# Layer 0 self attention: queries and keys from seven block products a step instead of eight, with sums formed in PSUM

## The chip, the cores and the metric

One core of a Trainium2 chip runs the whole kernel. The metric is the device time of one execution in microseconds (us). Five engines matter: TensorE (PE in the profile, its weight loads PEld), VectorE (DVE), ScalarE (ACT), GpSimd (POOL) and SyncE (SP), which issues the transfers. Each works through its own list of instructions in order and waits on semaphores where it needs another's result. PSUM has eight banks of 512 fp32 columns; TensorE writes them, VectorE and ScalarE read them, and ScalarE can write them too.

## The reference

Two transformer layers over 16 sequences of 256 tokens with 256 features, all fp32. The part that the change touches is the self attention of layer 0: 16 heads of 64, rotary positions, no mask.

```
q = _heads(xq @ wq)
k, v = jnp.split(ctx @ wkv, 2, axis=-1)
...
q = _rope(q, sq, cq)
k = _rope(k, sk, ck)
sim = jnp.einsum('bhnd,bhmd->bhnm', q, k) * DH ** (-0.5)
a = jax.nn.softmax(sim, axis=-1)
o = jnp.einsum('bhnm,bhmd->bhnd', a, v)
return o @ wo + bo
```

In self attention `ctx` is `xq`, the normalized and modulated input, so queries and keys are both a product of the same 256 x 256 activations with 256 x 1024 weights.

## The kernel before, in words

Six phases follow each other: layer 0 self attention, cross attention, feed forward, then the same three of layer 1. A phase has one job for each of the 16 sequences. A layer 0 attention job has two steps, s = 0 and s = 1 (called the even and the odd step here); a step handles eight heads, as two groups of four (u = 2s and 2s + 1, or e = 0 and 1). The loop runs over all steps, and the order of every engine's instructions is the order in which the program issues them (a manual schedule), so a line that stands earlier in the loop body is ahead on its engine.

A step of layer 0 self attention, in the order of TensorE:

1. Scores (`scores`, L1057, and `stage_s`, L585; matmuls at L598) of this step into banks 0 to 3 (e = 0) and 4 to 7 (e = 1). ScalarE takes four exponentials (L610) out of them into `pr`.
2. Queries and keys of the next step (`stage_rotary`, L539, through `product`, L77, whose matmul is L82): for each of four pairs (e, half) one bank holds 256 columns of q and 256 of k. `product` cuts the 128 output rows into four strips of 32, which TensorE works on side by side. Each bank is multiplied on VectorE with cosines and with sines (L555, two instructions of 512 columns), and once both halves of an e are there, GpSimd joins them into `qk` (L563, two instructions of 512 columns). The products `m0` and `m1` have two buffers each.
3. Attention-weighted values (`layer0_sums`, L659, matmuls L667), copied out by ScalarE (L674).
4. In the even step the values of the next job (`layer0_values`, L487, 64 matmul instructions of 512 columns); in the odd step the output projection of the job before (`finish_folded`, L946), which already works with seven block products of 128 columns and adds its results onto x on VectorE (L958, L959, L961, L964, L965). It uses banks 4 and 5.

VectorE also sums the exponentials (`stage_t`, L619: the two key halves of `pr`, both in SBUF, are added; `stage_turn`, L625, a transpose; `stage_reduce`, L632), and does the normalization of a later job (L349 to L373). GpSimd also scales the attention results (`scale`, L656, four instructions of 512 columns, in the even step), forms five sums for the output projection (`fold_inner`, L944: three in the even step after `scale`, two in the odd step between the two pairs of L563), adds a bias (L451) and half of the input's affine (L425). One fp32 matmul of the program shows as two instructions in the profile.

Weights: `wk0`, `wq0`, `wk1`, `wq1` hold the two halves of the key and query weights, `wo` the output weights (two slots under this tag). `load_phase(p, part)` issues a phase's loads by parts; the output weights belong to "early", which for phase p + 1 is issued in the second job of phase p.

Of the kernel before, what the change touches and what calls it, by code (L numbers as in the profile page):

```python
# [10 lines left out]
F32 = mybir.dt.float32  # L11
I32 = mybir.dt.int32
AF = mybir.ActivationFunctionType
ALU = mybir.AluOpType
AX = mybir.AxisListType

P = 128
# [26 lines left out]
def fast(ctx: ExitStack, tc: tile.TileContext, a: dict, out: bass.AP, flag):  # L44
# [222 lines left out]
    def wtile(shape, tag, name, bufs=1):  # L267
        return wpool.tile(shape, F32, tag=tag, name=name, bufs=bufs)
# [4 lines left out]
    def load_layer0_attention(kind, part, between=None):  # L273
        halves = [slice(i * 512, (i + 1) * 512) for i in range(4)]
        wkv_src = chunked(a[f"{kind}_wkv"])
        w = {}
        if part in ("first", "last"):
            i = ("first", "last").index(part)
            wk, wq = (wtile([P, 2, 512], f"w{n}{i}", f"w{n}{i}_{kind}") for n in "kq")
            nc.sync.dma_start(out=wk, in_=wkv_src[:, :, halves[i]])  # L280
            nc.sync.dma_start(out=wq, in_=chunked(a[f"{kind}_wq"])[:, :, halves[i]])
            w[f"wk{i}"], w[f"wq{i}"] = wk, wq
            if between is not None and i == 0:
                between()
        if part == "values":
            w["wv"] = wtile([P, 2, H * 64], "wv", f"wv_{kind}")
            for i in range(2):
                nc.sync.dma_start(out=w["wv"][:, :, halves[i]], in_=wkv_src[:, :, halves[2 + i]])
        if part == "early":
            w["bo"] = broadcast_row(a[f"L0_xcond_{kind}_bo"], "bo", f"bo_{kind}")  # L290
            w["wo"] = wtile([P, 8, D], "wo", f"wo_{kind}", 2)
            nc.sync.dma_start(out=w["wo"], in_=chunked(a[f"{kind}_wo"]))
        return w
# [245 lines left out]
    def stage_rotary(job, u, half, first_bank):  # L539
# [18 lines left out]
        if half == 1:  # L558
            (even_cos, even_sin), (odd_cos, odd_sin) = job["turns"]
            job["turns"] = []  # L560
            for out, (x, y) in enumerate(((even_cos, odd_sin), (odd_cos, even_sin))):
                r = work.tile([P, 2, N], F32, tag="qk", name=f"qk_{key}_{u}_{out}", bufs=4)
                nc.gpsimd.tensor_tensor(r, x, y, (ALU.subtract, ALU.add)[out])  # L563
                job["qk"].setdefault(u, []).append(r)

    def stage_a(job, c, at):

        w, key = job["phase"]["w"], job["key"]
        cut = slice(c * P, (c + 1) * P)
        pq = bank(at, 2, N)  # L570
        for s, (wt, src) in enumerate(((w["wq"], job["hT"]), (w["wk"], job["kT"]))):
            for k in range(2):
                product(pq[:, s, :], wt[:, k, cut], src[:, k, :], k == 0, k == 1)
        q = work.tile([P, N], F32, tag="ctx", name=f"q_{key}_{c}")
        nc.vector.tensor_scalar(q, pq[:, 0, :], w["bq"](c), None, ALU.add)

        k1 = work.tile([P, 2, N], F32, tag=("both", "squares")[c], name=f"k_{key}_{c}", bufs=1)
        nc.vector.scalar_tensor_tensor(
            k1, pq[:, 1:2, :].to_broadcast([P, 2, N]), w["bk"](c),
            mask[:, 0:2].rearrange("p (e o) -> p e o", o=1).to_broadcast([P, 2, N]), ALU.add, ALU.mult,  # L580
        )
        for e in range(2):
            job["qk"][2 * c + e] = (q, k1[:, e, :])

    def stage_s(job, u, at):  # L585

        key = job["key"]
        pair = job["qk"].pop(u)
        for t in range(NT):
            for half in range(2 if job["layer"] == 0 else 1):  # L590
                for g, h in [(g, h) for g in range(2) for h in range(4)]:
                    r = slice(32 * h, 32 * h + 32)
                    keys = slice(t * P + 64 * g, t * P + 64 * g + 64)
                    if job["layer"] == 0:
                        lhs, rhs = pair[half][r, 1, keys], pair[half][r, 0, :]
                    else:
                        lhs, rhs = pair[1][r, keys], pair[0][r, :]
                    nc.tensor.matmul(  # L598
                        banks[64 * g : 64 * g + 64, at + h, t * N : (t + 1) * N], lhs, rhs,
                        start=(half == 0), stop=(half == 1 or job["layer"] == 1),  # L600
                    )
        prs = []
        for p in range(2):
            pr = work.tile([P, 2, NT, N], F32, tag="pr", name=f"pr_{key}_{u}_{p}", bufs=4)
            sc = banks[:, at + 2 * p : at + 2 * p + 2, :].rearrange("p h (t n) -> p h t n", n=N)

            parts = 2 if job["layer"] == 1 and u % 2 == 0 and p == 0 else 1
            for i in range(parts):
                one = slice(i, i + 1) if parts == 2 else slice(0, 2)
                nc.scalar.activation(pr[:, one], sc[:, one], AF.Exp, scale=0.125 if job["layer"] == 0 else 0.25)  # L610
            prs.append(pr)
        job["pr"][u] = prs
# [43 lines left out]
            nc.gpsimd.tensor_tensor(part, part, spread[:, u : u + 1, :].to_broadcast([P, 2, N]), ALU.mult)  # L656
            job["parts"].append(part)

    def layer0_sums(job, u, at):  # L659

        key, v, prs = job["key"], job["v"], job["pr"].pop(u)
        o = bank(at, 2, N)
        for half in range(2):
            for t in range(NT):
                for h in range(4):
                    col = (4 * u + h) * 64 + 32 * half
                    nc.tensor.matmul(  # L667
                        o[32 * h : 32 * h + 32, half, :], v[:, t, col : col + 32], prs[h // 2][:, h % 2, t, :],
                        start=(t == 0), stop=(t == NT - 1),
                    )  # L670
        if u % 2 == 0:
            job["halves"].append(work.tile([P, 4, N], F32, tag="part", name=f"raw_{key}_{u}", bufs=4))
        raw = job["halves"][-1][:, 2 * (u % 2) : 2 * (u % 2) + 2, :]
        nc.scalar.copy(raw, o)  # L674
        job["raw"].append(raw)
# [267 lines left out]
            folded[m] = work.tile([P, 4, P], F32, tag="folded", name=f"folded_{job['key']}_{m}", bufs=5)  # L943
            eng.tensor_tensor(folded[m], *sums[m])  # L944

    def finish_folded(job, at):  # L946

        x, weights, hidden = xs[job["b"]], job["phase"]["folded"], job.pop("folded")
        hurry = len(at) == 3
# [3 lines left out]
        for m in (3, 6, 4, 5, 2, 1, 7) if hurry else places:  # L953
# [7 lines left out]
        nc.vector.tensor_tensor(  # L961
            square, first[:, 2:4, :].unsqueeze(1).to_broadcast([P, 2, 2, P]), square, ALU.add
        )
        nc.vector.tensor_tensor(outer, third[:, 0:1, :].to_broadcast([P, 2, P]), outer, ALU.add)  # L964
        nc.vector.tensor_tensor(outer, second[:, 1:3, :], outer, ALU.add)  # L965
        if job["last"]:
# [90 lines left out]
    def scores(i):  # L1057

        at0, at1 = attention(i, 0), attention(i, 1)
        if at0:  # L1060
            for e in range(2):
                stage_s(at0[0], 2 * at0[1] + e, 4 * e)
        if at1:
            for e in range(2):
                stage_s(at1[0], 2 * at1[1] + e, 4 * ((e + at1[1]) % 2))
        then = attention(i + 1, 0)
        if then and then[0]["cross"]:
            for e in range(2):
                start_keys(then[0], 2 * then[1] + e, 2 * e)
# [5 lines left out]
    phases[0]["make_mod"] = phases[0]["mod_load"]()  # L1075
    load_x(0)
    nc.sync.dma_start(out=rows, in_=a["rows"])
    for part in ("first", "last", "early"):
        load_phase(0, part)
    for b in range(3, NB):  # L1080
        load_x(b)
# [26 lines left out]
    add_bias(jobs[0])  # L1108
    prepare_moments(jobs[2])
    prepare_norm(jobs[2])  # L1110
    prepare_input(jobs[1])
    for i, (j, s) in enumerate(steps):
        job = jobs[j]
        ffn, layer0 = job["kind"] == "ffn", job["layer"] == 0
# [13 lines left out]
        leaving = layer0 and not ffn and job["b"] == NB - 1  # L1128
        if layer0 and not ffn and job["b"] == NB - 2 and s == 1:
            load_phase(job["p"] + 1, "values")  # L1130
        if leaving and s == 0:
            load_phase(job["p"] + 1, "first")
        if layer0 and not ffn and s == 1 and job["b"] == 2:
# [100 lines left out]
        elif layer0:  # L1234
            then = attention(i + 1, 0)
            if leaving and s == 1 and nxt["kind"] == "ffn":
                fold_input_weights(nxt["phase"], nc.gpsimd)
            stage_t(job, 2 * s, 0)
            stage_t(job, 2 * s, 1)
            stage_turn(job, 2 * s)  # L1240
            rotary(then, 0, 0)
            stage_t(job, 2 * s + 1, 0)
            rotary(then, 0, 1)
            if late is not None and s == 1 and then:
                fold_inner(late, nc.gpsimd, 7, 6)
            if late is not None and s == 0:
                sum_up(late, 6)
            if make_mod:
                make_mod["mod"] = make_mod["make_mod"](6)
            stage_t(job, 2 * s + 1, 1)  # L1250
            rotary(then, 1, 0)
            rotary(then, 1, 1)
            if leaving and s == 0:
                load_phase(job["p"] + 1, "last")
            for e in range(2):
                layer0_sums(job, 2 * s + e, 4 + e if then else e)
            stage_reduce(job, 2 * s)
            stage_turn(job, 2 * s + 1)
            stage_reduce(job, 2 * s + 1)
            if late is not None and s == 1:  # L1260
                if then:
                    finish_folded(late, (4, 5))
                else:
                    finish(late, 7)
            if late is not None and s == 0:
                scale(late)
                if nxt["kind"] == "attn":
                    fold_inner(late, nc.gpsimd, 5, 2, 1)
            if nxt["kind"] == "attn" and s == 0:
                layer0_values(nxt)  # L1270
            if s == 0:
                prepare_moments(third)
                context_moments(third)
                prepare_fetch(after)
            else:
                prepare_norm(third)
                prepare_context(third)
                prepare_input(after)
# [652 lines left out]
```

## Time and profile before

| | us |
|---|---|
| Runs of the kernel before | 2176.7, 2177.61, 2177.8; median 2177.61 |
| The profiled execution's own time | 2174.7 |
| Its span, from first to last instruction | 2172.9 |
| Granted TensorE clock, mean | 0.999 |
| First and last matmul with `wk_sa` (layer 0 self attention) | 12.3 and 649.3 |

The profile lists busy times by engine, groups of instructions by line, a timeline, and the chain of work that ended last. In a row, "x128" is a count, "128x512" partitions by columns, and what stands after "<-" in brackets is what ended the engine's idle time. A matmul row's busy time overlaps with its neighbours', since matmuls are pipelined; where a duration of a stretch of matmuls is needed, it is taken from one start to the next.

### The profile page before, as it was taken

The page shows a single profiled execution, that of the slowest core. Times are in us where ns is not written, and L with a number is a line of the kernel's source. Part 1 is how long each engine was busy: PE and PEld are TensorE (multiplying, and loading weights), DVE is VectorE, ACT ScalarE, POOL GpSimd, SP SyncE. Part 2 cuts the span into 40 slices and gives each one's busy share as a digit, 9 for nine tenths or more (in the row PEclk, how much of TensorE's full clock was granted, in tenths as well). Part 3 has the DMA queues.
Part 4 walks back from the last instruction along what each step waited for, and adds up shares of the span by engine and source line. Part 5 has one row for each costly group of instructions (what it writes and reads, how often), then busy time and mean ns, then how long its engine had stood idle before and what let it go on. Part 6 is the DMA issues. An engine that isn't in the chain of part 4 may idle for free.

```text
span 2172.9 us, 110193 instructions
## 1 busy us (share of the span) xinstructions
PE 2154.7 (99%) x50112; PEld 1437.1 (66%) x50112; DVE 1688.5 (78%) x3108; ACT 870.1 (40%) x1362; POOL 1240.9 (57%) x1174
## 2 busy tenths in 40 slices
PE   9999999999999999999999999999999999999998
PEld 5666666666665666666666667998556665656787
DVE  6876777777888889888889887774777777777875
ACT  3323233233233233332333334443666666664432
POOL 3766656656657867677676767662232323235673
PEclk9999999999999999999999999999999999999999
DMA  6110010011123221121211123221211232223221
GB/s 194 49 38 22 23 42 22 23 29 36 27 74 86 66 58 44 42 60 35 61 41 44 43 62 99 56 44 25 64 43 39 48 102 63 59 48 78 74 64 39
DMA packets 307030, 117.69 MB, mean 54 GB/s; under 512 B 243364, under 2 KB 289784, under 8 KB 306424
## 3 DMA queue, kind: packets, MB, share of 16 engines
q1 hardware_dynamic: 306008, 110.02, 20.5%
q8 instruction: 394, 6.46, 1.3%
q14 instruction: 84, 0.69, 0.1%
q10 hardware_dynamic: 544, 0.52, 0.1%
HBM read 77.14 MB, written 33.29 MB: 51 GB/s over the span
## 4 chain that ended last, share of the span: by engine, by line
PE 92%; POOL 2%; DVE 2%; DMA 2%; issue 1%; SPq 1%; ACT 0%; DVEq 0%; POOLq 0%; ACTq 0%
PE banks L82 59%; PE banks L598 16%; PE banks L667 9%; PE banks L683 5%; PE banks L534 1%; PE banks L501 1%; POOL raw L656 1%; DMA spread<-sums_seen 0%; DVE m L555 0%; DMA fetched<-turned 0%; DMA sums_seen<-inv 0%; SPq L388 0%; POOL qk L563 0%; POOL folded L944 0%; POOL folded L869 0%
## 5 line engine op out<-in xcount | busy, mean ns | idle before, releaser
L610 ACT ACTIVATE pr<-banks 128x1024 f32<-128x1024 f32 x576 | 487.4, 937 | 415.3 <-PE banks L598 211.9
L563 POOL TENSOR_TENSOR qk<-m,m 128x512 f32<-128x512 f32 x256 | 347.8, 1379 | 302.6 <-DVE m L555 210.7
L555 DVE TENSOR_TENSOR m<-banks,rope 128x512 f32<-128x512 f32 x512 | 324.2, 679 | 85.7 <-POOL qk L563 81.4
L619 DVE TENSOR_TENSOR both<-pr 128x512 f32<-128x512 f32 x256 | 218.9, 867 | 107.9 <-ACT pr L610 107.5
L674 ACT COPY raw<-banks 128x512 f32<-128x512 f32 x128 | 75.2, 587 | 467.3 <-PE banks L667 443.1
L598 PE MATMUL banks<-qk 32*64 32x256 f32 x8192 | 240.7, 377 | 3.0 <-DVE x L961 1.8
L667 PE MATMUL banks<-pr,v 128*32 128x256 f32 x4096 | 233.2, 379 | 0.0
L598 PEld LDWEIGHTS banks<-qk 32*64 32x64 f32 x8192 | 184.1, 131 | 63.7 <-issue 22.4
L667 PEld LDWEIGHTS banks<-pr,v 128*32 128x32 f32 x4096 | 132.9, 110 | 88.7 <-ACT pr L610 0.7
L656 POOL TENSOR_TENSOR raw<-raw,spread 128x512 f32<-128x512 f32 x128 | 162.7, 1304 | 19.7 <-DMA spread<-sums_seen 19.3
L725 POOL TENSOR_TENSOR oT<-oT,spread 128x256 f32<-128x256 f32 x64 | 45.8, 737 | 206.0 <-DVE spread L724 206.0
L625 DVE STREAM_TRANSPOSE squares<-both 128x1024 f32<-128x1024 f32 x128 | 159.4, 1246 | 4.4
L632 DVE TENSOR_REDUCE rows<-squares 128x32 f32<-128x1024 f32 x128 | 155.4, 1214 | 2.2
L451 POOL TENSOR_TENSOR x<-x,bo_b 128x256 f32<-128x256 f32 x96 | 73.0, 781 | 121.2 <-DVE xh L363 121.2
L82 PE MATMUL banks<-hT,wk_sa 128*32 128x256 f32 x2048 | 134.7, 381 | 0.0
L683 PE MATMUL banks<-pr,wide_v 128*32 128x256 f32 x2048 | 134.3, 379 | 0.0
L82 PE MATMUL banks<-hT,wq_ca 128*32 128x256 f32 x2048 | 133.9, 379 | 0.0
L82 PE MATMUL banks<-hT,wq_sa 128*32 128x256 f32 x2048 | 133.9, 379 | 0.0
L355 POOL TENSOR_TENSOR rstd<-ve,neg_half 128x2 f32<-128x2 f32 x95 | 73.0, 769 | 101.0 <-DVE ve L353 97.6
L944 POOL TENSOR_TENSOR folded<-raw,raw 128x512 f32<-128x512 f32 x90 | 127.8, 1448 | 2.4
L900 DVE TENSOR_TENSOR x<-banks,x 128x256 f32<-128x256 f32 (+2 forms) x150 | 79.7, 531 | 63.2 <-PE banks L82 57.0
L598 PE MATMUL banks<-q,k 32*64 32x256 f32 x4096 | 127.8, 381 | 0.0
(225 smaller groups left out, 4020.8 us busy)
## 6 DMA issues: line engine op xcount, KB each, us to landing
turned<-blocks SPq DMA_DIRECT2D x380, 64.0 KB
fetched<-turned SPq DMA_DIRECT2D x380, 64.0 KB
spread<-sums_seen SPq DMA_DIRECT2D x128, 128.0 KB
x<-in_x SPq DMA_DIRECT2D x16, 256.0 KB
fetched_c<-turned_c SPq DMA_DIRECT2D x64, 64.0 KB
cT<-in_ctx_turned SPq DMA_DIRECT2D x16, 256.0 KB
out<-x SPq DMA_DIRECT2D x15, 256.0 KB
ctx<-in_ctx SPq DMA_DIRECT2D x16, 192.0 KB
```

Source lines behind the costliest of these rows:

```text
L82: nc.tensor.matmul(out[cut], lhsT[:, cut], rhs, start=start, stop=stop, **more)
L555: nc.vector.tensor_tensor(m, pq, rope[:, s : s + 1, :].to_broadcast([P, 2, N]), ALU.mult)
L563: nc.gpsimd.tensor_tensor(r, x, y, (ALU.subtract, ALU.add)[out])
L598: nc.tensor.matmul(banks[64 * g : 64 * g + 64, at + h, t * N : (t + 1) * N], lhs, rhs, start=(half == 0), stop=(half == 1 or job["layer"] ...
L610: nc.scalar.activation(pr[:, one], sc[:, one], AF.Exp, scale=0.125 if job["layer"] == 0 else 0.25)
L619: nc.vector.tensor_tensor(job["both"][:, 2 * p : 2 * p + 2, :], pr[:, :, 0, :], pr[:, :, 1, :], ALU.add)
L625: nc.vector.transpose(job["squares"].rearrange("p b k -> p (b k)"), job.pop("both").rearrange("p h n -> p (h n)"))
L632: nc.vector.tensor_reduce(job["rows"][:, u, :], job.pop("squares"), AX.X, ALU.add)
L656: nc.gpsimd.tensor_tensor(part, part, spread[:, u : u + 1, :].to_broadcast([P, 2, N]), ALU.mult)
L667: nc.tensor.matmul(o[32 * h : 32 * h + 32, half, :], v[:, t, col : col + 32], prs[h // 2][:, h % 2, t, :], start=(t == 0), stop=(t == NT - 1),
L683: nc.tensor.matmul(o[32 * h : 32 * h + 32], v[:, t, 4 * c + h, 32 * e : 32 * e + 32], prs[h // 2][:, h % 2, t, :], start=(t == 0), stop=(t ...
L944: eng.tensor_tensor(folded[m], *sums[m])
```

## The change

For the steps of layer 0 self attention of jobs 1 to 15 (30 steps; job 0 keeps the old way for its own two), the product of 256 tokens x 256 features with 256 features x 256 columns is done as a 2 x 2 block product with seven instead of eight products of 128 x 128 blocks, for each of two halves of q and of k.

- `fold_projections` forms the weight sums: 8 instructions of 128x512 for a step index, once; for s = 0 on GpSimd ahead of the loop, for s = 1 on VectorE in the odd step of job 0. The sum `low[0] + low[1]` replaces a part of the weights in place.
- `fold_tokens` forms four sums of 128x128 of a job's input on GpSimd, in the even step of the job before, ahead of `scale`.
- `begin_seven` issues products 1 and 5 (banks 0 and 1) right after the scores, and ScalarE copies bank 0 to bank 2 between the third and the fourth exponential. The other products are added onto banks 0, 1 and 2 in the order 2, 6, 7, 4, 3, between the quarters of `layer0_sums`. `keep_sum` (ScalarE) copies bank 2 to SBUF after product 6 and after product 7; `add_fifth` (VectorE) adds bank 1 to each copy.
- `rotate` replaces the rotary part: again two VectorE instructions of 128x512 for each of four pieces, but a piece is now one token half of one e. Two pieces come from PSUM (banks 0 and 2), two from the SBUF copies. GpSimd joins each piece with two instructions of 128x256.
- The scores start their PSUM accumulation once in a bank instead of twice. In the odd step `stage_reduce` of the second group moves between the third and the fourth of the five additions of `finish_folded`. `sum_up` comes after product 6, and `fold_inner` 7 and 6 stand ahead of all `rotate` work on GpSimd.
- `sums_of_weights` takes the second slot of `wo`, so the output weights of the cross attention are loaded by a new part "output" in the odd step of job 15 instead of job 1.

```diff
+    def fold_projections(ph, s, eng):
...
+            eng.tensor_tensor(s3[:, i], top[0], low[0], ALU.subtract)
+            eng.tensor_tensor(low[0], low[0], low[1], ALU.add)
+            eng.tensor_tensor(s2[:, i], low[0], top[0], ALU.subtract)
+            eng.tensor_tensor(s4[:, i], top[1], s2[:, i], ALU.subtract)
...
+    def fold_tokens(job, eng):
...
+        eng.tensor_tensor(t1, b[0][1], b[0][0], ALU.subtract)
+        eng.tensor_tensor(t2, b[1][1], t1, ALU.subtract)
+        eng.tensor_tensor(t3, b[1][1], b[0][1], ALU.subtract)
+        eng.tensor_tensor(t4, b[1][0], t2, ALU.subtract)
...
+    def seven(job, s, m, place, start=False):
+        for i, n in enumerate("qk"):
+            a = job["phase"]["projections"][s][n][m]
+            for half in range(2):
+                product(
+                    place[:, 2 * i + half, :], a[:, half * P : (half + 1) * P], job["tokens"][m],
+                    start and i == 0 and half == 0, True, skip_group_check=True,
+                )
+    def begin_seven(job, s):
+        first, fifth, chain = (bank(i, 4, P) for i in range(3))
+        seven(job, s, 1, first, True)
+        seven(job, s, 5, fifth, True)
+        nc.scalar.copy(chain, first)
+    def keep_sum(job, s, i):
...
+            kept = work.tile([P, 4, P], F32, tag="cT", name=f"kept{i}_{key}_{s}")
+        nc.scalar.copy(kept, bank(2, 4, P))
+        return kept
+    def add_fifth(kept):
+        nc.vector.tensor_tensor(kept, bank(1, 4, P), kept, ALU.add)
+    def rotate(job, s, e, t, src):
...
+        for i in range(2):
+            m = work.tile([P, 4, P], F32, tag=f"m{i}", name=f"m{i}_{key}_{u}_{t}")
+            nc.vector.tensor_tensor(m, src, rope[:, i : i + 1, t * P : (t + 1) * P].to_broadcast([P, 4, P]), ALU.mult)
...
+        for i, r in enumerate(job["qk"][u]):
+            nc.gpsimd.tensor_tensor(
+                r[:, :, t * P : (t + 1) * P], cos[:, i], sin[:, 1 - i], (ALU.subtract, ALU.add)[i]
+            )
...
-            stage_t(job, 2 * s, 0)
-            stage_t(job, 2 * s, 1)
-            stage_turn(job, 2 * s)
-            rotary(then, 0, 0)
-            stage_t(job, 2 * s + 1, 0)
-            rotary(then, 0, 1)
...
+            if by_seven(then):
+                ahead = then
+                first, fifth, chain = (bank(n, 4, P) for n in range(3))
+                for p in range(2):
+                    stage_t(job, 2 * s, p)
+                stage_turn(job, 2 * s)
+                if late is not None and s == 1:
+                    fold_inner(late, nc.gpsimd, 7, 6)
...
+                stage_t(job, 2 * s + 1, 0)
+                layer0_sums(job, 2 * s, 4, (0,))
+                seven(*ahead, 2, first)
+                rotate(*ahead, 0, 0, first)
+                seven(*ahead, 6, chain)
+                two = keep_sum(*ahead, 0)
+                if late is not None and s == 0:
+                    sum_up(late, 6)
+                stage_reduce(job, 2 * s)
+                layer0_sums(job, 2 * s, 4, (1,))
+                stage_t(job, 2 * s + 1, 1)
+                layer0_sums(job, 2 * s + 1, 5, (0,))
+                seven(*ahead, 7, chain)
+                three = keep_sum(*ahead, 1)
+                layer0_sums(job, 2 * s + 1, 5, (1,))
+                seven(*ahead, 4, chain)
+                add_fifth(three)
+                rotate(*ahead, 1, 1, three)
+                seven(*ahead, 3, fifth)
+                add_fifth(two)
+                rotate(*ahead, 0, 1, two)
+                rotate(*ahead, 1, 0, chain)
...
+                stage_turn(job, 2 * s + 1)
+                if late is None or s == 0:
+                    stage_reduce(job, 2 * s + 1)
...
-                    finish_folded(late, (4, 5))
+                    finish_folded(late, (4, 5), (lambda: stage_reduce(job, 3)) if by_seven(then) else None)
...
             if late is not None and s == 0:
+                if job["p"] == 0 and not nxt["cross"]:
+                    fold_tokens(nxt, nc.gpsimd)
                 scale(late)
```

## The prediction

> **What bounds the kernel now.** I read the page's busy shares first, then the busy times of one job of the changed phase (an even and an odd step) stretch by stretch, then the chain of waits there, then the rows of the instructions that the change adds or moves.
>
> ```profile
> PE 2154.7 (99%) x50112; PEld 1437.1 (66%) x50112; DVE 1688.5 (78%) x3108; ACT 870.1 (40%) x1362; POOL 1240.9 (57%) x1174
> ```
> ```profile
> 309.23:330.30 21.07, 21.07 (x397) 11.16 (x393) 16.50 (x28) 6.70 (x9) 12.43 (x11) 1.00 0.21 53
> 330.30:350.55 20.25, 20.25 (x549) 15.16 (x545) 14.36 (x19) 6.03 (x8) 12.87 (x11) 1.00 0.01 3
> sum 41.32, PE 41.32 PEld 26.33 DVE 30.86 ACT 12.74 POOL 25.30; mean PE 20.66 PEld 13.16 DVE 15.43 ACT 6.37 POOL 12.65
> ```
> ```profile
> 303.19 6.11 PE banks L82 x224
> 309.30 3.64 PE banks L598 x128
> ...
> 334.01 7.04 PE banks L82 x128
> 341.05 3.45 PE banks L667 x64
> ```
>
> The columns of the second fence are length, then busy time and count of PE, PEld, DVE, ACT and POOL. A job takes 41.32 us, and TensorE is busy for all of it: VectorE has 10.5 us free, GpSimd 16.0. In the chain, all of this stretch is PE. So whatever shortens PE's list counts, until another engine is late.
>
> **The change, part by part.** *Products.* A step's queries and keys were 128 instructions of 256 columns, 6.92 us from first start to the next kind's (333.94 to 340.87 in the timeline). Now they are 7 x 32 = 224 instructions of 128 columns. The third fence has this very shape and count: the output projection, 224 in 6.11 us, with weight loads of the same size. So 6.92 - 6.11 = 0.8 saved a step. The same 96 of 128 columns once took 2.73, 28.4 ns each: 6.37, saving 0.55. I take 0.8, as the longer stretch has it. 30 steps: 24 us is all that can be won.
>
> *ScalarE* gets three copies of 512 columns a step, 0.59 each from the row of L674 (PSUM to SBUF). PSUM to PSUM is not in the trace; the bounds are 0.59 and, by the row of the exponential of 1024 columns, 1.03. I take 0.59: even the other adds 0.44 behind an engine that is busy 12.7 of 41.3.
>
> *VectorE* gets two additions a step (bank and SBUF, 512 columns: 0.69, row of L961). The eight multiplications stay eight of 512 columns, but four now read both operands in SBUF. Before, all read PSUM and the table. This is where I see the price. The rows:
>
> ```profile
> L555 DVE TENSOR_TENSOR m<-banks,rope x512: 650/680/694, 14.3 to 1274.6; 128x512 f32<-128x512 f32 x171
> L619 DVE TENSOR_TENSOR both<-pr x256: 620/680/1819, 29.3 to 1285.0; 128x512 f32<-128x512 f32 x128
> L944 POOL TENSOR_TENSOR folded<-raw,raw x90: 1265/1287/1835, 86.6 to 1247.7; 128x512 f32<-128x512 f32 x90
> L725 POOL TENSOR_TENSOR oT<-oT,spread x64: 729/737/746, 1526.1 to 1971.7; 128x256 f32<-128x256 f32 x64
> ```
> ```profile
> 85.23 1.29 POOL L656 TENSOR_TENSOR raw<-raw,spread 128x512 f32<-128x512 f32 x1
> ...
> 85.57 3.19 DVE L619 TENSOR_TENSOR both<-pr 128x512 f32<-128x512 f32 x2 [1.50 <-ACT pr L610]
> ...
> 86.60 3.30 POOL L944 TENSOR_TENSOR folded<-raw,raw 128x512 f32<-128x512 f32 x2
> ```
>
> L555 (one operand in PSUM) never passes 694 ns. L619 (both in SBUF) is 680 by median and 1819 at worst, and its long ones lie where GpSimd works: two took 3.19 us instead of 1.29, while two L944 took 3.30 instead of 2.53. Each waits for the other's instruction to end: some 0.6 lost by GpSimd's, up to 1.1 by VectorE's. The four multiplications from SBUF join L619 in this, with GpSimd more loaded.
>
> The Trainium skill, "SBUF — State Buffer", "Who interferes with whom", states it as a rule that speaks against this change: a VectorE instruction with two SBUF inputs and a GpSimd instruction contend for a port pair that is locked for a whole instruction. As an estimate from that page, with each of eight such instructions waiting for one whole GpSimd instruction (four of 1.29, four of 0.74), the sum below would have L = 8.1 in place of the one used.
>
> *GpSimd.* Joining: 16 instructions of 256 columns a job at 0.74 for 8 of 1.29 (+1.5). `fold_tokens`: four of 128 columns, not in the trace; between 0.2 (the 128-column memset) and 0.74; I take 0.47, the line through 0.74 and 1.29 carried on, 1.9 a job. What is worse is the order. Before, the even step's train of `scale`, three sums and rstd began ahead of the odd step's scores and ended 4.4 us before the next joining:
>
> ```profile
> 325.48 5.00 POOL L656 TENSOR_TENSOR raw<-raw,spread 128x512 f32<-128x512 f32 x4
> 330.56 3.74 POOL L944 TENSOR_TENSOR folded<-raw,raw 128x512 f32<-128x512 f32 x3
> 334.25 1.17 POOL L355 TENSOR_TENSOR rstd<-ve,neg_half 128x2 f32<-128x2 f32 x1
> 339.84 2.84 POOL L563 TENSOR_TENSOR qk<-m,m 128x512 f32<-128x512 f32 x2 [4.42 <-DVE m L555]
> ```
>
> Now the last `rotate` follows products 4 and 3 and `fold_tokens` follows it, so the train starts some 5 us later, and the two sums 7 and 6 are queued ahead of all joining.
>
> *The odd step, laid out.* I set each engine's list end to end with start-to-start times from the timeline (0.60 for VectorE's 512 columns, 1.17 transpose, 1.14 reduce, 1.24 and 0.70 on GpSimd), 0.25 from a matmul's last start to a reader and 0.05 between others. The same way the job before gives 41.2 (profile: 41.32). Times count from the step's scores.
>
> - TensorE: 3.64 scores, 6.11 products, 3.46 values, 6.11 projection: 19.3 to the next scores, 21.2 to their second group, which writes bank 5.
> - VectorE starts at 3.1, after the first exponential (3.1 in the timeline too). Four L619 2.4, two transposes 2.3, two reduces 2.3, eight multiplications 4.8, two additions 1.3, then the five additions of the projection 2.3: 15.4. It waits 0.5 for the second copy and 0.8 for GpSimd to release `m0` and `m1`: 19.8 without lost turns.
> - Turns lost to GpSimd, L: 0.8 and 1.1 in the first two L619, 0.6, 1.1, 0.5 and 0.5 in the four multiplications: 4.7. With them the last addition out of bank 5 ends at 24.5.
>
> So the scores' second group waits 24.5 - 21.2 = 3.3 us for bank 5, where it waited for nothing. (The first group waits 1 us of this for the late joining.) The even step has the same SBUF pairs, but 20.3 us of TensorE and neither projection nor normalization behind them: VectorE ends in time. A job: -1.6 + 3.3 = +1.7 to 1.8. In general it is L - 2.9. I bound L by 0 and by 8 x 1.1 = 8.7 (all as long as the worst rows), and take 4.7, where the lists fall against each other.
>
> *Once.* Weight sums on GpSimd: 8 x 1.24 plus turns = 10.9 from 29.45, its idle stretch ends at 36.23; the input for the values is then ready at 40.8, TensorE wants it at 40.2: +0.7. Odd step of job 0: no projection covers the joining, so the scores wait 4.2 and 0.8 is saved: +3.4. Its eight sums on VectorE (5 us) make it late in the next step: `add_fifth`, behind which product 3 waits, is 3 us late, +3.4. Together +7.5; bounds 3.4 (the second alone) and 12 (GpSimd's sums uncovered).
>
> *At nothing:* the scores' start flags (same matmuls); the moved `stage_reduce` (in the sum); the later load of `wo_ca`, 1 MB on SP ahead of that step's other transfers, which by the 194 GB/s of the page's first slice is 5.4 us, and is needed some 30 us later. If that cover goes, 5.4 once.
>
> **Sum.** 14 jobs' odd and even steps from the first odd one on: 14 x 1.8 = 25, plus 7.5: +33 us. On the profiled execution's 2174.7 (span 2172.9) that is 2207.7; the median of the runs is 2.9 above it, so **2210 us**.
>
> **Rivals.** *TensorE stays the bound* (not slower). If L is under 1.3, no scores wait, and a job gains 1.6: -22 + 6 to 7.5, **2161 us**. For it: VectorE's busy 30.9 of 41.3 plus 2.8 leaves room on paper, and half of the L619 have no wait (median 680). Against: the train on GpSimd now lies under the odd step's list. It decides at L = 2.4, where the gain of 14 jobs pays the 7.5. *Balance*: L of 2.4 to 3, some turns missed: **2178 us**. *GpSimd becomes the bound*: if the 256-column joining and 128-column sums cost 0.8 and 0.55 instead of 0.74 and 0.47, the train ends later, the second pair of `m` is held longer, and a job costs 3 to 3.5: **2232 us**. That the products' pitch falls short (28.4 ns) adds 0.25 a step to any case; it makes no case of its own.
>
> **Chances.** Forecast (TensorE waits for VectorE's bank 5) 0.62; TensorE stays the bound 0.18; balance 0.10; GpSimd the bound 0.10. A measurement of this kernel tells about 0.2% (4.4 us) from no change, so faster 0.18, same 0.10, slower 0.72. The range 2168 to 2232 leaves out most of the first rival and half of the last, under 0.2 together; L's outer bound of 8.7 (2270 us) gets next to nothing.
>
> **What would show it.** Right: a job of some 43 us; PE idle at L598 ended by VectorE's x of the projection's last two additions or by GpSimd's joining; multiplications from SBUF near 1.1 to 1.8 us where those from PSUM stay at 0.68; the `scale` train running past the odd step's scores. Wrong: a job of 39.7 with PE without gaps, or SBUF multiplications at 0.68 beside a working GpSimd. The forecast fails if the copies in SBUF and the table do not take turns with GpSimd as L619 does, or if the lists fall differently against each other. Products: 224 instructions a step at 27.3 ns; much more than 28.4 refutes the 0.8.

## The result, and the profile after

| | before | after |
|---|---|---|
| Median of the runs, us | 2177.7 (4 runs, 2176.7 to 2177.95) | 2211.89 (4 runs, 2207.08 to 2213.25) |
| Profiled execution, us (span) | 2174.7 (2172.9) | 2207.08 (2205.3) |
| From the first scores to those of step 30 (counted from 0), us | 613.57 | 645.53 |

The changed kernel is slower: ratio 1.0154 [1.0136, 1.0171]. Nearly all of it (32.0 of 32.4 us in the profiled executions) lies in the 30 steps that the change touches.

The page's busy shares, after:

```profile
PE 2152.0 (98%) x52992; PEld 1471.8 (67%) x52992; DVE 1805.7 (82%) x3176; ACT 923.7 (42%) x1452; POOL 1332.6 (60%) x1362
```

TensorE has 2880 instructions more and is 2.7 us less busy, VectorE has 68 more and is 117 us busier. The 60 additions of `add_fifth` at 0.68 us and the eight weight sums at 0.42 are 44 us: the other 73 are instructions that have become longer.

The same stretches as before, an odd and an even step of one steady job (length, then busy time and count of PE, PEld, DVE, ACT and POOL, then the granted clock):

```profile
304.48:325.34 20.86, 19.80 (x644) 16.99 (x640) 17.98 (x21) 7.73 (x11) 20.16 (x19) 1.00 0.02 4
325.34:347.64 22.30, 21.09 (x492) 13.01 (x489) 20.56 (x32) 8.59 (x12) 11.15 (x16) 1.00 0.21 51
sum 43.16, PE 40.89 PEld 30.00 DVE 38.54 ACT 16.32 POOL 31.31; mean PE 20.45 PEld 15.00 DVE 19.27 ACT 8.16 POOL 15.65
```

A job takes 43.16 us, where it took 41.32. PE is no longer busy for all of it, and GpSimd is busy for 20.16 of the odd step's 20.86 us. (A matmul's busy time runs on past the next one's start; start to start, TensorE's list is 39.6 of the 43.2, so about 3.5 us of a job are waits.)

Where those waits are stands in the timeline of PE in the changed kernel (start, duration, line; in brackets the idle time and what ended it):

```profile
316.51 0.65 PE L82 MATMUL banks<-tokens,wk_sa 128*32 128x128 f32 x16
318.22 1.08 PE L82 MATMUL banks<-hT,sums_of_weights 128*32 128x128 f32 x32 [1.06 <-DVE kept L628]
...
325.34 2.49 PE L679 MATMUL banks<-qk 32*64 32x256 f32 x66
329.05 1.98 PE L679 MATMUL banks<-qk 32*64 32x256 f32 x62 [1.21 <-DVE x L1054]
```

The first is product 3, which writes bank 1 and so waits for `add_fifth` (L628) to have read it. From 316.51, 0.43 us are work until the next start, so it starts 1.28 late. The second is the scores' second group, which waits for the last addition out of bank 5 (L1054). It starts 3.71 after the first, whose 66 instructions take 1.88 of the scores' 3.64: 1.83 late.

The timeline of VectorE in the odd step leads to both:

```profile
307.59 3.42 DVE L703 TENSOR_TENSOR both<-pr 128x512 f32<-128x512 f32 x2 [2.50 <-ACT pr L694]
...
312.39 1.55 DVE L703 TENSOR_TENSOR both<-pr 128x512 f32<-128x512 f32 x1
...
316.20 1.37 DVE L703 TENSOR_TENSOR both<-pr 128x512 f32<-128x512 f32 x1
317.49 0.68 DVE L628 TENSOR_TENSOR kept<-banks,kept 128x512 f32<-128x512 f32 x1
318.27 2.11 DVE L637 TENSOR_TENSOR m<-kept,rope 128x512 f32<-128x512 f32 x2
...
321.08 2.28 DVE L637 TENSOR_TENSOR m<-kept,rope 128x512 f32<-128x512 f32 x2
323.29 1.27 DVE L637 TENSOR_TENSOR m<-banks,rope 128x512 f32<-128x512 f32 x2
...
328.57 0.42 DVE L1054 TENSOR_TENSOR x<-banks,x 128x256 f32<-128x256 f32 x1
```

Two multiplications from PSUM (`m<-banks`) take 1.27 us. Two from SBUF take 2.11 and 2.28, and the four `stage_t` (L703) 3.42, 1.55 and 1.37, where 0.68 is one undisturbed. From 311 on VectorE has no gap worth naming: it is late because of what it has to run, and each of these long rows has both operands in SBUF. GpSimd in the same time:

```profile
305.03 5.43 POOL L740 TENSOR_TENSOR raw<-raw,spread 128x512 f32<-128x512 f32 x4
310.54 4.55 POOL L1031 TENSOR_TENSOR folded<-raw,raw 128x512 f32<-128x512 f32 x3
315.06 0.69 POOL L356 TENSOR_TENSOR rstd<-ve,neg_half 128x2 f32<-128x2 f32 x1
315.73 2.96 POOL L1031 TENSOR_TENSOR folded<-raw 128x512 f32<-128x512 f32 x2
318.66 4.16 POOL L643 TENSOR_TENSOR qk<-m,m 128x256 f32<-128x256 f32 x4
```

It works without a pause from 305.03 to 322.82, and its instructions are stretched too: three sums 4.55 instead of 3 x 1.29, four joinings 4.16 instead of 4 x 0.74.

The groups by line over the whole kernel (count, then ns min/median/max):

```profile
L637 DVE TENSOR_TENSOR m<-banks,rope x120: 672/678/694, 53.6 to 690.5; 128x512 f32<-128x512 f32 x120
L637 DVE TENSOR_TENSOR m<-kept,rope x116: 683/1131/1766, 58.4 to 668.6; 128x512 f32<-128x512 f32 x116
L703 DVE TENSOR_TENSOR both<-pr x256: 621/862/1850, 28.2 to 1319.8; 128x512 f32<-128x512 f32 x128
L1031 POOL TENSOR_TENSOR folded<-raw,raw x90: 1267/1614/1784, 95.1 to 1282.5; 128x512 f32<-128x512 f32 x90
```

One line of code, one shape, one table as the second operand: 678 ns by median with the first operand in PSUM, 1131 with it in SBUF. `stage_t`, which the change didn't edit, went from 680 to 862 by median, and the sums on GpSimd from 1287 to 1614.

### The profile page after: what moved, and what is told of

Same layout as the page of the kernel before. It is cut to its first block, busy times and chain, and to the rows that moved or that the text cites. A ratio compares the mean times of both kernels' runs of the same rounds, so it can differ in the third digit from the quotient of the medians.

```text
span 2205.3 us, 116296 instructions
## 1 busy us (share of the span) xinstructions
PE 2152.0 (98%) x52992; PEld 1471.8 (67%) x52992; DVE 1805.7 (82%) x3176; ACT 923.7 (42%) x1452; POOL 1332.6 (60%) x1362
## 4 chain that ended last, share of the span: by engine, by line
PE 74%; DVE 15%; POOL 5%; issue 3%; DMA 1%; ACT 1%; SPq 0%; DVEq 0%; POOLq 0%; ACTq 0%
PE banks L82 47%; PE banks L679 13%; PE banks L751 7%; PE banks L770 5%; DVE m L637 5%; DVE both L703 3%; DVE squares L709 2%; PE banks L535 1%; PE banks L502 1%; POOL folded L956 1%; POOL folded L1031 1%; POOL raw L740 1%; DVE rows L716 1%; DVE kept L628 1%; ACT pr L694 1%
## 5 line engine op out<-in xcount | busy, mean ns | idle before, releaser
L694 ACT ACTIVATE pr<-banks 128x1024 f32<-128x1024 f32 x576 | 492.5, 936 | 487.7 <-PE banks L679 380.0
L703 DVE TENSOR_TENSOR both<-pr 128x512 f32<-128x512 f32 x256 | 267.2, 1061 | 55.8 <-ACT pr L694 52.4
L679 PE MATMUL banks<-qk 32*64 32x256 f32 x8192 | 255.1, 380 | 26.6 <-DVE x L1054 17.9
L643 POOL TENSOR_TENSOR qk<-m,m 128x256 f32<-128x256 f32 x240 | 194.7, 840 | 131.3 <-DVE m L637 126.4
L564 POOL TENSOR_TENSOR qk<-m,m 128x512 f32<-128x512 f32 x136 | 184.8, 1380 | 134.5 <-DVE m L556 115.4
L751 PE MATMUL banks<-pr,v 128*32 128x256 f32 x4096 | 244.6, 379 | 0.0
L556 DVE TENSOR_TENSOR m<-banks,rope 128x512 f32<-128x512 f32 x272 | 172.3, 679 | 48.8 <-POOL qk L564 45.8
L740 POOL TENSOR_TENSOR raw<-raw,spread 128x512 f32<-128x512 f32 x128 | 169.2, 1355 | 13.9 <-DMA spread<-sums_seen 12.4
L508 ACT COPY v<-banks 128x512 f32<-128x512 f32 x128 | 70.4, 593 | 170.4 <-PE banks L82 107.0
L1031 POOL TENSOR_TENSOR folded<-raw,raw 128x512 f32<-128x512 f32 x90 | 135.7, 1535 | 2.4
```

The lines of the kernel that those rows point to most:

```text
L556: nc.vector.tensor_tensor(m, pq, rope[:, s : s + 1, :].to_broadcast([P, 2, N]), ALU.mult)
L643: nc.gpsimd.tensor_tensor(r[:, :, t * P : (t + 1) * P], cos[:, i], sin[:, 1 - i], (ALU.subtract, ALU.add)[i])
L679: nc.tensor.matmul(banks[64 * g : 64 * g + 64, at + h, t * N : (t + 1) * N], lhs, rhs, start=(half == 0 and (t == 0 or job["layer"] == 1)) ...
L703: nc.vector.tensor_tensor(job["both"][:, 2 * p : 2 * p + 2, :], pr[:, :, 0, :], pr[:, :, 1, :], ALU.add)
L751: nc.tensor.matmul(o[32 * h : 32 * h + 32, half, :], v[:, t, col : col + 32], prs[h // 2][:, h % 2, t, :], start=(t == 0), stop=(t == NT - 1),
```

## The experiments

Theory: a VectorE instruction with both operands in SBUF and a GpSimd instruction take turns; the new SBUF operands and the later GpSimd train bring more such pairs into the odd step, VectorE gets late, and PE waits for `add_fifth` and bank 5. Rivals: (1) VectorE simply has too many instructions; (2) the order on GpSimd and the two buffers of `m` do it, without any taking of turns.

**e1_psum: `add_fifth` writes its sum into PSUM.** The multiplications then read a bank. Count and order of instructions stay as they are. In the odd step all four pieces then come from a bank, in the even step three (the expectation below counts three for the odd step, but takes off the losses of all four SBUF multiplications).

```diff
-    def add_fifth(kept):
-        nc.vector.tensor_tensor(kept, bank(1, 4, P), kept, ALU.add)
+    def add_fifth(kept, at=None):
+        total = kept if at is None else bank(at, 4, P)
+        nc.vector.tensor_tensor(total, bank(1, 4, P), kept, ALU.add)
+        return total
...
-                add_fifth(three)
+                three = add_fifth(three, 7 if s == 1 else None)
...
-                add_fifth(two)
+                two = add_fifth(two, 3)
```

> The two VectorE additions of bank 1 write their sums to PSUM (bank 3 in every step, bank 7 in odd steps) instead of SBUF, so three of the four pieces' multiplications in an odd step read PSUM; the number of instructions on every engine is the same. Theory (VectorE instructions with two SBUF operands take turns with GpSimd): L in the odd step falls by the 1.8 us that its four SBUF multiplications lost in the changed kernel (0.3, 0.5, 0.5, 0.5 over 680 ns), GpSimd's joining gets faster too, a job falls from 43.16 to 40.6-41.4 and the time to 2176-2188. Rival 1 (VectorE has too much to do, whatever its operands): job 43.2, time 2212 as the changed kernel. Rival 2 (the late GpSimd train alone holds the buffers m): job within 0.5 of 43.2.

Measured: 2175.73 against 2175.45 for the kernel before, ratio 1.0001 [0.9992, 1.0011]; 36 us less than the changed kernel. Its multiplications, and the same two steps of a job:

```profile
L639 DVE TENSOR_TENSOR m<-banks,rope x210: 672/680/696, 53.9 to 657.1; 128x512 f32<-128x512 f32 x105
L639 DVE TENSOR_TENSOR m<-kept,rope x28: 682/692/1216, 79.2 to 612.4; 128x512 f32<-128x512 f32 x28
```
```profile
292.31:312.64 20.33, 19.81 (x644) 16.97 (x640) 16.91 (x22) 7.74 (x11) 19.20 (x19) 1.00 0.02 4
312.64:333.17 20.53, 20.53 (x493) 13.05 (x489) 18.78 (x31) 8.56 (x12) 10.36 (x15) 1.00 0.21 55
```

The 210 never pass 696 ns, and the even step's PE has no gap. A job is 40.86 us. VectorE, too, can write a bank: the additions into PSUM take 0.69 us by median. VectorE's busy time in a job is 2.85 us less with the same list. Rival 1 falls. What is left in the odd step are the long `stage_t` (1185, 1769, 1556 and 1358 ns).

**e2_noscale: GpSimd's `scale` left out in this phase.**

```diff
-            nc.gpsimd.tensor_tensor(part, part, spread[:, u : u + 1, :].to_broadcast([P, 2, N]), ALU.mult)
+            if job["p"] > 0:
+                nc.gpsimd.tensor_tensor(part, part, spread[:, u : u + 1, :].to_broadcast([P, 2, N]), ALU.mult)
```

> Leaves out the four multiplications by the inverse sums on GpSimd in the self attention of layer 0 (the attention there stays unnormalized); VectorE's list is untouched. Theory: the GpSimd train under the odd step is 5 us shorter, L falls from 5.5 to 2-3, a job takes 40-40.7, time about 2172-2180. Rival 1 (VectorE's amount of work): job 43.2, time 2207-2213. Rival 2 (GpSimd's train holds the buffers m): also faster, but with VectorE's SBUF multiplications as long as before (1.0-1.2 us).

Measured: 2165.86 (one run), beyond the fast end of what was expected. From the first scores to those of step 30 it takes 610.2, so 35.3 of the 41 us that it gains on the profiled changed kernel lie there; the rest lies behind those steps and was not followed. A job is 40.6 us. The multiplications still read SBUF:

```profile
L637 DVE TENSOR_TENSOR m<-kept,rope x116: 682/695/1225, 58.2 to 630.5; 128x512 f32<-128x512 f32 x116
```

Same operands and the same VectorE list, but 695 instead of 1131 ns: the length comes from what GpSimd runs beside it. Rival 2 had them stay long, which does not fit. Either half of the pair, taken away, gives the loss back.

**e3_early and e4_psum_early: the train earlier.** In e3 `fold_tokens` moves to the start of the even step (its tile gets four slots), so that `scale` is not behind it; e4 is e3 with e1's edit.

```diff
+                if late is not None and s == 0 and not nxt["cross"]:
+                    fold_tokens(nxt, nc.gpsimd)
                 for p in range(2):
...
             if late is not None and s == 0:
-                if job["p"] == 0 and not nxt["cross"]:
-                    fold_tokens(nxt, nc.gpsimd)
                 scale(late)
```

> The four token sums on GpSimd are formed at the start of the even step, where GpSimd waits 3.9 us for VectorE, instead of ahead of scale at its end (four slots instead of two). Same instructions. Theory: the train starts 1.9 us earlier, so it meets less of the odd step's SBUF pairs: job 41.2-42.2, time 2190-2200. Rival 1: no change, 2212.

> Both edits, sums in PSUM and early token sums. Theory: VectorE is in time for bank 5, TensorE is nearly without a wait, job 39.8-40.3, time 2166-2174, faster than the kernel before by the products' 0.8 us a step less the start. Rival 1: 2212.

Measured: e3 2189.4, ratio 1.0064 [1.0047, 1.0081], a job of 41.8; e4 2165.58, ratio 0.9952 [0.9935, 0.9968], a job of 40.3. Four instructions of 0.46 us, taken from ahead of the train, are worth 22 of the 34 us that the change costs: where GpSimd's work lies matters beside the operands, which were worth 36.

**e5_between: `stage_reduce` back behind the five additions.** In the changed kernel it takes 1.2 us of VectorE ahead of the last two additions out of bank 5.

```diff
-                    finish_folded(late, (4, 5), (lambda: stage_reduce(job, 3)) if by_seven(then) else None)
+                    finish_folded(late, (4, 5))
+                    if by_seven(then):
+                        stage_reduce(job, 3)
```

> The changed kernel with one part undone: the reduce of the second group stands again behind the five additions of the projection, not between the third and the fourth. Nothing else moves. Theory: the scores' second group waits for bank 5, which the last two additions hold; they end 1.2 us earlier, so a job falls by 1.0-1.2 to about 42 and the time by 14-17 to 2195-2198. Rival 1 (VectorE's amount of work sets the job, not the hold on bank 5): the list is as long as before, 2212. Rival 2 (the GpSimd train sets it): 2212.

Measured: 2198.46, ratio 1.0108 [1.009, 1.0125], half a microsecond above the expected range; the odd step stays at 20.86, the even one falls from 22.30 to 21.40. The scores' second group, in PE's timeline, now starts 2.81 behind the first instead of 3.71:

```profile
320.93 2.50 PE L679 MATMUL banks<-qk 32*64 32x256 f32 x66
323.74 1.55 PE L679 MATMUL banks<-qk 32*64 32x256 f32 x48 [0.32 <-DVE x L1054]
```

So bank 5 is what the even step waits for, and work put ahead of its release costs directly: 13 us.

**e6_all: e4, with sums 7 and 6 behind the first joining on GpSimd** (the two lines of `fold_inner(late, nc.gpsimd, 7, 6)` moved behind `rotate(*ahead, 0, 0, first)`).

> The early token sums and the sums in PSUM, and the projection's sums 7 and 6 on GpSimd behind the first joining, as in the kernel before, instead of ahead of it. Theory: with the waits nearly gone the joining comes earlier and an odd step loses another 0.1-0.3 us: 2162-2167. Rival 2 (the place of 7 and 6 holds the buffers m and is the main cost): 2155 or less.

Measured: 2162.4, ratio 0.994 [0.9922, 0.9958]; a job of 40.0. Against e4 the order of the sums gives 3 us by the medians, less than the 5 us over which e4's own runs spread; by the two traces a job is 0.3 shorter. Rival 2, in this form, is small.

**e7_before_sbuf and e10_copies_only: the effect without the change.** Both start from the kernel before. In jobs 1 to 12, ScalarE copies each bank of queries and keys to SBUF. In e7 the multiplications read the copy, in e10 they go on reading the bank.

```diff
+        src = pq
+        if job["p"] == 0 and 0 < job["b"] < NB - 3:
+            src = work.tile([P, 2, N], F32, tag="cT", name=f"seen_{key}_{u}_{half}")
+            nc.scalar.copy(src, pq)
...
-            nc.vector.tensor_tensor(m, pq, rope[:, s : s + 1, :].to_broadcast([P, 2, N]), ALU.mult)
+            nc.vector.tensor_tensor(m, src, rope[:, s : s + 1, :].to_broadcast([P, 2, N]), ALU.mult)
```

(In e10 the copy is called `seen`, and `src` stays `pq`.)

> The kernel before, with eight products, but for jobs 1 to 12 of layer 0 self attention ScalarE copies every bank of queries and keys to SBUF and VectorE multiplies from there: the same VectorE and GpSimd instructions, other operands. Theory: the multiplications from SBUF are 0.68 us where GpSimd rests and up to 1.8 where it works; joining on GpSimd gets longer as well (1.29 to 1.7). There is 10 us of free time on VectorE in a job, so the time stays within 2175-2195. Rival 1 (operands don't matter): every multiplication 0.68 and 2176.

> Control for the kernel before with multiplications from SBUF (2215): the same copies by ScalarE to SBUF, in the same jobs 1 to 12, but the multiplications read PSUM again and nothing reads the copies. Theory (SBUF operands take turns with GpSimd): multiplications at 0.68, odd step at 20.25, even at 21.07, 2175-2182. Rival (the copies, by their time on ScalarE or by holding the banks, made the 37 us): 2200-2215.

Measured: e7 2215.1, e10 2176.14 (one run each), the kernel before, measured beside them, 2176.23 and 2175.74. e7's expectation missed by 20 us, upward. Its multiplications, and then e10's:

```profile
L559 DVE TENSOR_TENSOR m<-banks,rope x320: 651/680/696, 13.3 to 1313.1; 128x512 f32<-128x512 f32 x160
L559 DVE TENSOR_TENSOR m<-seen,rope x192: 647/684/1780, 52.7 to 569.0; 128x512 f32<-128x512 f32 x192
```
```profile
L559 DVE TENSOR_TENSOR m<-banks,rope x512: 650/681/695, 13.9 to 1274.1; 128x512 f32<-128x512 f32 x171
```

These two kernels have the same instructions in the same order; only where eight multiplications a step read differs, and that is 39 us. The copies alone cost nothing. In e7 the odd steps stay at 20.25, and the even ones go from 21.07 to 23.44 or 25.06, again with PE waiting for an addition out of a bank. The expectation had counted VectorE's 10 us of free time in a job; but the long multiplications stand ahead of the five additions, so their length delays the release of the banks, whatever is free elsewhere. A median of 684 ns hides it: mean 969, maximum 1780.

**e11_sbuf_noscale: e7 with `scale` left out**, as in e2.

> The kernel before with multiplications from SBUF in jobs 1 to 12, and the four multiplications by the inverse sums on GpSimd left out in the self attention of layer 0 (the attention there stays unnormalized). VectorE and ScalarE do the same as at 2215. Theory: less of GpSimd to take turns with: the even step falls from 23.4-25.1 to 21-22.5, time 2177-2195. Rival (VectorE's detour by SBUF itself, whatever GpSimd does): 2210-2215.

Measured: 2187.22 (one run). The even steps fall to 22.23, the odd ones stay at 20.25. From the first scores to those of step 30 the three kernels take 613.9 (e10), 653.4 (e7) and 630.2: 23 of e7's 39.5 us go with `scale`. The others, by the rows, stay with the joining and sums 7 and 6, which GpSimd runs beside the second four multiplications (no run took these away); the timelines of VectorE and GpSimd in this kernel:

```profile
308.94 5.74 DVE L559 TENSOR_TENSOR m<-seen,rope 128x512 f32<-128x512 f32 x4 [1.17 <-POOL qk L567]
```
```profile
310.11 3.42 POOL L949 TENSOR_TENSOR folded<-raw 128x512 f32<-128x512 f32 x2
```

Four take 5.74 us, where the four ahead of GpSimd's work took 2 x 1.29.

**e8_nofold: the odd half's weight sums left out** (the eight VectorE instructions behind `if s == 0`).

> The changed kernel without the eight weight sums of the odd half on VectorE (the odd half's products then use the even half's sums, so its queries and keys are wrong). Theory on the start: the step after the first odd one takes 24.1 us instead of 21.1 because these sums make VectorE late; without them 21.1-21.5, the step before stays at 17.0, the time falls by 2.5-4. If the weight sums on GpSimd or the missing projection are the start's cost, the step stays at 24.

Measured: 2206.28 (one run). Step 2 takes 22.4 instead of 24.11 us, more than expected; the two steps behind it together 1.4 us less. So the sums cost 3.1 us within the 30 steps (642.3 instead of 645.5). The whole execution is only 0.8 us shorter than the profiled changed kernel, less than the 2.5 to 4 expected; what takes the rest back behind the 30 steps was not followed. What stays in step 2 is told in the last section.

**e9_late: the best parts together.** e6 and e5, the seven products only from job 2 on, and the odd half's weight sums on GpSimd in job 1's odd step, where the projection covers them.

```diff
-        return then is not None and then[0]["p"] == 0 and then[0]["b"] > 0
+        return then is not None and then[0]["p"] == 0 and then[0]["b"] > 1
...
-                if job["p"] == 0 and job["b"] == 0:
-                    fold_projections(job["phase"], 1, nc.vector)
+                if job["p"] == 0 and job["b"] == 1:
+                    fold_projections(job["phase"], 1, nc.gpsimd)
```

> A version meant to beat both: sums in PSUM, early token sums, sums 7 and 6 behind the first joining, the reduce behind the five additions, and seven products only from job 2 on, with the odd half's weight sums on GpSimd in the odd step of job 1. Theory: two steps lose 0.8 each, the start's 6 us go (the first odd step is 14.1 again, the next 21.1): 2157-2162. If the weight sums disturb job 2 as much as they did job 1: 2164.

Measured: 2158.97 against 2175.74, ratio 0.9923 [0.9907, 0.994]: the fastest of all. Its job:

```profile
282.30:301.80 19.50, 19.50 (x644) 16.94 (x640) 16.52 (x21) 7.73 (x11) 17.50 (x17) 1.00 0.02 4
301.80:322.20 20.40, 20.40 (x498) 13.07 (x494) 19.07 (x31) 8.41 (x12) 12.64 (x17) 1.00 0.24 56
sum 39.90, PE 39.90 PEld 30.02 DVE 35.59 ACT 16.14 POOL 30.14; mean PE 19.95 PEld 15.01 DVE 17.79 ACT 8.07 POOL 15.07
```

PE is busy throughout again, and a job is 1.4 us shorter than before: the products' saving is real once VectorE no longer holds the banks.

## Why the prediction was right, point by point

**The products: right.** 32 instructions of 128 columns every 0.87 us, so seven take 6.1; 0.8 a step was called. With the waits gone a job is 39.9, near the 41.3 - 1.6 = 39.7 of the rival in which TensorE stays the bound.

**The mechanism: right**, and shown from both sides (e1 and e7 with e10 for the operands, e2 and e11 for GpSimd). The Trainium skill, "SBUF — State Buffer", "Who interferes with whom", agrees here: two SBUF inputs contend with GpSimd, and the page says that one SBUF input does not. The second half is the 694 to 696 ns maximum of every `m<-banks` group above. That the two engines slow each other down is shown; that one always waits for the other's whole instruction is not, since no run separates this from a finer sharing.

**L, the turns lost in the odd step: under-sized.** Called 4.7 for two `stage_t` and four multiplications (its six terms add up to 4.6). Measured in the odd step: the four `stage_t` 1726, 1767, 1554 and 1369 ns, the four multiplications 975, 1217, 1139 and 1214; with 680 taken off each, 3.7 + 1.8 = 5.5. The second group's `stage_t` lose 1.6 and were called at nothing, since their place beside the sums on GpSimd was not seen; the multiplications lose 1.8, not 2.7. The estimate from the page, a whole GpSimd instruction for each of eight, was 8.1.

**The waits for `m0` and `m1` (0.8): not there.** In the timeline the multiplications at 321.08 and 323.29 follow with no wait. The 0.5 for the second copy is not a wait there either; short gaps between the instructions make up about as much. So the last addition out of bank 5 ends at 328.99 - 304.48 = 24.5, as called, but from a list 0.8 shorter and turns 0.8 longer: that the two errors cancel is luck. A job is L - 3.7, not L - 2.9. e1 fits: L falls to 3.1 (its `stage_t` alone), which gives 40.7, and 40.86 is measured.

**The wait for bank 5 (3.3): half of it lies elsewhere.** This is the step that failed. I had `add_fifth` in time for product 3; the two long `stage_t` ahead of it make product 3 start 1.28 late. The next scores begin at 20.9; called were 20.3, with 1 us of waiting for GpSimd's joining, a wait that isn't there. Their second group waits 1.83. Together that is 3.1 for the 3.3 called, because bank 5 is released at the same time whichever wait comes first; e5 shows that this release is what counts.

**A job: +1.84, called +1.8.** Eleven steady jobs lie between 43.13 and 43.19.

**The start: 7.5 called.** Step 0 costs nothing (0.7 called). Step 1 costs 2.9 (3.4 called): PE waits 3.5 us for GpSimd's joining, and 0.8 is saved. Step 2 costs 3.0 (3.4 called), but of other parts: product 3 starts some 1.7 late, and about 2.1 come from a slower clock, which I didn't foresee. Steps 3 and 4 cost 1.5 more than a steady job; e8 takes 1.4 of that away, so the odd half's weight sums reach further than the one step that I gave them. Sum: 7.4, in part by other terms than mine, so its closeness to 7.5 is luck too.

**GpSimd as the bound: the prices were not the cause.** Tokens take 0.457 each (0.47 called) and joining 0.736 by median (0.74 called). Its odd step is nearly full, 20.16 of 20.86 us, but some 3 us of that are stretched rows: its four trains above take 5.43, 4.55, 2.96 and 4.16, where the same instructions undisturbed take 5.00 and 3.74 (before), 2.53 (e2) and 2.81 (e1). The list as a whole is 19.20 in e1.

**The copies and the terms at nothing:** ScalarE's copies take 0.586 from a bank to SBUF and 0.571 from bank to bank (0.59 called); TensorE's weight loads wait for those of `keep_sum` 15 times, 4.9 us in the whole kernel. The later load of `wo_ca` and the scores' start flags were not tried by themselves; the 0.4 us outside the 30 steps leaves little room for the load, and the scores' 128 matmuls take 3.71 us in both kernels.

## What to carry to other kernels

When an edit moves a VectorE operand from PSUM to SBUF, ask whether the instruction now reads two operands in SBUF and what GpSimd runs at that moment: here that alone cost 39 us in a kernel that was otherwise the same, and writing a sum to PSUM instead of SBUF (0.69 us for an addition instead of 0.68) was worth 36. The trace before shows it in the maximum of a group, not its median, and in the rows of both engines laid side by side. And where an engine is late, look at which bank it releases last: 1.2 us of movable work ahead of that release was worth 13 us.

## What the runs showed of the hardware that was not expected

**TensorE's clock falls after a gap.** In the changed kernel PE idles for 3.5 us at the end of step 1. The scores behind the gap, and the stretches in and after it (the clock is the third number from the right):

```profile
63.14 5.78 PE L679 MATMUL banks<-qk 32*64 32x256 f32 x128 [3.54 <-POOL qk L643]
```
```profile
59.60:63.14 3.54, 0.00 (x0) 0.00 (x1) 3.44 (x6) 0.00 (x0) 2.63 (x4) 1.00 0.00 0
64.00:67.00 3.00, 3.00 (x68) 2.66 (x63) 2.90 (x5) 0.19 (x1) 1.15 (x2) 0.51 0.01 3
67.00:70.00 3.00, 3.00 (x106) 2.55 (x94) 2.86 (x9) 2.77 (x3) 0.28 (x1) 0.92 0.02 5
```

The clock is about half for some 3 us, and the scores there take 5.78 instead of 3.71 us. So a wait of 3.5 us cost 5.6. That these 2.1 us are what e8 leaves in step 2 (20.3 of list + 2.1 = 22.4) is read off the rows (e8 has the same gap and the same 5.78 us of scores); no run took the gap alone away. The Trainium skill, "TensorE: Matmul & The Clock Gate", "What's actually happening", has the clock at half after an idle window of about 3.4 us; this gap agrees.

**The clock also fell after shorter gaps, but not each time.** In e7 PE's timeline has idle times of 1.19 and 0.31 us, and the clock is this:

```profile
332.13 0.61 PE L602 MATMUL banks<-qk 32*64 32x256 f32 x2 [1.19 <-DVE x L965]
333.06 3.53 PE L602 MATMUL banks<-qk 32*64 32x256 f32 x62 [0.31 <-DVE x L969]
```
```profile
332.00:335.00 3.00, 2.56 (x42) 1.72 (x50) 2.85 (x7) 0.95 (x2) 1.60 (x3) 0.72 0.00 0
```

Such an even step takes 25.06 us, and one without the fall 23.44, with the same waits (1.21 and 0.31 us in the step from 285.26, with the clock at 1.00). In the changed kernel's steady jobs idle times of 1.06 and 1.21 us left the clock at 1.00. So whether these gaps cause the fall, and what decides, was not settled. Four of e7's ten steady even steps have it, 1.6 us each: some 6.5 of the 20 us by which its expectation missed.
